# Layer 0's x and adjacency: transposed on TensorE, or loaded again as 32x32 blocks and turned on VectorE

## Chip, core and metric

The kernel runs on one core of one Trainium2 chip. The metric is the device time of an execution in microseconds (us). Engines are named as in the profile: PE (TensorE, PEld its weight loads), DVE (VectorE), ACT (ScalarE), POOL (GpSimd) and SP (SyncE, which issues the DMAs).

## What is computed

128 graphs of 128 nodes with 512 features each, float32, go through two graph attention layers with 8 heads of 64. `x` is [128, 128, 512], `adj` is [128, 128, 128].

```python
# layer 0
Q, K, V = x @ W_q + b_q, x @ W_k + b_k, x @ W_v + b_v          # split into 8 heads
scores = Q K^T / sqrt(64) + (x @ w_g[:D])[:, :, None] + (x @ w_g[D:])[:, None, :] + b_g + log(adj + 1e-9)
x = softmax(scores) V + x
# layer 1
q, k, v = x @ Wq.T + bq, x @ Wk.T + bk, x @ Wv.T + bv
logits = q k^T / sqrt(64) + log(max(adj, 1e-8))
out = (softmax(logits) v) @ Wo.T + bo
x = layer_norm(x + out) * gamma + beta
```

## The kernel before

**Groups and steps.** The work goes in groups of G = 4 graphs, 32 groups. For every group and layer `proj_units` makes the projections (features on the partitions for q and k, nodes on the partitions for v), and `attn_units` the attention of each of the four graphs: `part1` computes the scores of 8 heads, transposed (keys on the partitions), the exponential on ACT (L216) and the product with the transposed adjacency on DVE (L223), so that the log becomes a factor; `part2` does the weighted sum with a column of ones for the denominator (L233) and divides (L250 to L257); `part3`, in layer 1 only, transposes the result (L272), multiplies by Wo (L277), adds x1 (L279) and does the layer norm, with its statistics and scaling on DVE (L305, L307, L311) and the rest on POOL (L309, L310, L312, L313), and stores the graph's output.

**The order.** The loop at L290 has one step for each group `s`, in two halves. In the first half the projections of group `s` in layer 0 are merged, unit by unit, with the attention of group `s - 2` in layer 1; then group `s + 1` is loaded (`load`); in the second half the projections of group `s - 1` in layer 1 are merged with the attention of group `s` in layer 0. This is the order in which the program is written. A scheduler then orders each engine's instructions, by dependence and its own estimates, and hands out the buffers of the pools; each engine works through its own list in that order, and an instruction that waits holds up all behind it on its engine.

**Transposes of the inputs.** The projections need x with features on the partitions, and the product at L223 needs the adjacency transposed. In `transposed` PE turns four 128x128 blocks of x into a PSUM tile (`ptx`, L123), and DVE copies the tile to `xT` (L124): four such units per group and layer. `adjacency` (layer 0 only) turns the four graphs' adjacency (`padj`, L129), and DVE reads that PSUM tile twice, into the two layers' factors in `adjT` (L131, L132). In layer 1, L123 and L124 transpose x1, the result of layer 0.

**Buffers.** `xT` has two buffers, which both layers share; `x` has two, `adj` two, `adjT` three. PSUM: two buffers `tr` for transposes, two `proj` for projections, Wo and v, one for the scores, one for the weighted sums.

**DMA.** SP issues all loads and stores. Group 0 is loaded first, then the weights and biases, then the other groups as buffers come free.

After the groups a count of good denominators decides whether a general path runs again; with these inputs it doesn't.

Of the kernel before, what the change touches and what calls it, by code (L numbers as in the profile page):

```python
# [8 lines left out]
F32 = mybir.dt.float32  # L9
# [3 lines left out]
AX = mybir.AxisListType  # L13
PSUM = bass.MemoryType.PSUM

H, P, G = 8, 128, 4
EPS0, ADJ_MIN, LN_EPS = 1e-9, 1e-8, 1e-5


# [3 lines left out]
def merged(a, b):  # L23

    order = [((i + 0.5) / len(a), 0, u) for i, u in enumerate(a)]
    order += [((i + 0.5) / len(b), 1, u) for i, u in enumerate(b)]
    return [u for _, _, u in sorted(order, key=lambda x: x[:2])]


def weight(nc, pool, w, name):  # L30
    KC = w.shape[0] // P
    t = pool.tile([P, KC, w.shape[1]], F32, name=name)
    nc.sync.dma_start(t, w.rearrange("(c p) e -> p c e", p=P))
    return t
# [14 lines left out]
def fast_path(ctx, tc, args, GOOD):  # L49
# [9 lines left out]
    nc = tc.nc  # L59
    B, N, D = x.shape  # L60
    HD = D // H
    KC = D // P
    NG = B // G
# [4 lines left out]
    act = ctx.enter_context(tc.tile_pool(name="act", bufs=2))  # L68
    work = ctx.enter_context(tc.tile_pool(name="work", bufs=2))
    small = ctx.enter_context(tc.tile_pool(name="small", bufs=4))  # L70
    ps = ctx.enter_context(tc.tile_pool(name="ps", bufs=2, space=PSUM))

    X, ADJ, AT2 = {}, {}, {}

    def load(g):
        X[g] = act.tile([P, G, D], F32, tag="x", name=f"x_{g}")
        nc.sync.dma_start(X[g], x[g * G : (g + 1) * G].rearrange("b p d -> p b d"))
        ADJ[g] = act.tile([P, G, N], F32, tag="adj", name=f"adj_{g}")
        nc.sync.dma_start(ADJ[g], adj[g * G : (g + 1) * G].rearrange("b p j -> p b j"))

    ident = const.tile([P, P], F32, name="ident")
    make_identity(nc, ident)

    load(0)
    WQ, WK, BQ, BK, BV = {}, {}, {}, {}, {}
    WQ[0], WK[0] = weight(nc, const, w_q0, "wq0"), weight(nc, const, w_k0, "wk0")

# [13 lines left out]
    minus_half = const.tile([P, 1], F32, name="minus_half")  # L101
    nc.gpsimd.memset(minus_half, -0.5)

    XT, X1, QT, KT, V, AC, GATE, PT, AT, RC = {}, {}, {}, {}, {}, {}, {}, {}, {}, {}

    def proj_units(g, L):
        src = X if L == 0 else X1

        def start():
            XT[g, L] = act.tile([P, KC, G, N], F32, tag="xT", name=f"xT_{g}_{L}")  # L110
            QT[g, L] = act.tile([P, KC, G, N], F32, tag="qT", name=f"qT_{g}_{L}")
            KT[g, L] = act.tile([P, KC, G, N], F32, tag="kT", name=f"kT_{g}_{L}")
            V[g, L] = act.tile([P, G, H, HD + 1], F32, tag="v", name=f"v_{g}_{L}")
            nc.gpsimd.memset(V[g, L][:, :, :, HD : HD + 1], 1.0)
            if L == 0:
                AC[g] = small.tile([P, G, 2], F32, tag="ac", name=f"ac_{g}", bufs=2)

        def transposed(c):
            if c == 0:
                start()  # L120
            p = ps.tile([P, G, N], F32, tag="tr", name=f"ptx_{g}_{L}_{c}")
            for b in range(G):
                nc.tensor.transpose(p[:, b, :], src[g][:, b, c * P : (c + 1) * P], ident)  # L123
            nc.vector.tensor_copy(XT[g, L][:, c], p)  # L124

        def adjacency():
            p = ps.tile([P, G, N], F32, tag="tr", name=f"padj_{g}")
            for b in range(G):
                nc.tensor.transpose(p[:, b, :], ADJ[g][:, b], ident)  # L129
            AT2[g] = act.tile([P, 2, G, N], F32, tag="adjT", name=f"adjT_{g}", bufs=3)  # L130
            nc.vector.tensor_scalar_add(AT2[g][:, 0], p, EPS0)  # L131
            nc.vector.tensor_scalar_max(AT2[g][:, 1], p, ADJ_MIN)  # L132

        def qk(W, bias, dst, e):
            p = ps.tile([P, G * N], F32, tag="proj", name=f"pqk_{g}_{L}_{e}")
            for c in range(KC):
                nc.tensor.matmul(  # L137
                    p,
                    W[L][:, c, e * P : (e + 1) * P],
                    XT[g, L][:, c].rearrange("p b n -> p (b n)"),  # L140
                    start=(c == 0),
                    stop=(c == KC - 1),
                )
            nc.scalar.activation(  # L144
                dst[g, L][:, e].rearrange("p b n -> p (b n)"), p, AF.Identity, bias=bias[L][:, e : e + 1]
            )

        def v0(b, s):
            W2 = D // 2
            n = W2 + 2 * s  # L150
            p = ps.tile([P, W2 + 2], F32, tag="proj", name=f"pv_{g}_{L}_{b}_{s}")
            for c in range(KC):
                nc.tensor.matmul(  # L153
                    p[:, 0:n], XT[g, L][:, c, b], wv0[:, c, s * W2 : s * W2 + n],
                    start=(c == 0), stop=(c == KC - 1),
                )
            h2 = slice(s * H // 2, (s + 1) * H // 2)
            nc.vector.tensor_tensor(
                V[g, L][:, b, h2, 0:HD],
                p[:, 0:W2].rearrange("p (h d) -> p h d", d=HD),  # L160
                BV[L][:, s * W2 : (s + 1) * W2].rearrange("p (h d) -> p h d", d=HD),
                ALU.add,
            )
            if s == 1:
                nc.vector.tensor_copy(AC[g][:, b], p[:, W2:n])

        def v1(b):
            p = ps.tile([P, D], F32, tag="proj", name=f"pv_{g}_{L}_{b}")
            for c in range(KC):
                nc.tensor.matmul(p, XT[g, L][:, c, b], wv1[:, c], start=(c == 0), stop=(c == KC - 1))  # L170
            nc.vector.tensor_tensor(
                V[g, L][:, b, :, 0:HD],
                p.rearrange("p (h d) -> p h d", h=H),
                BV[L].rearrange("p (h d) -> p h d", h=H),
                ALU.add,
            )

        def gate():

            GATE[g] = small.tile([P, G, 1], F32, tag="gate", name=f"gate_{g}", bufs=2)  # L180
            nc.scalar.activation(GATE[g], AC[g][:, :, 0:1], AF.Exp, bias=bg)

        def add_bo():
            for b in range(G):
                nc.gpsimd.tensor_tensor(X1[g][:, b], X1[g][:, b], BO, ALU.add)

        u = [lambda c=c: transposed(c) for c in range(KC)]
        if L == 0:
            u += [adjacency]
        for e in range(KC):  # L190
            u += [lambda e=e: qk(WQ, BQ, QT, e), lambda e=e: qk(WK, BK, KT, e)]
        if L == 0:
            u += [lambda b=b, s=s: v0(b, s) for b in range(G) for s in range(2)]
            u += [gate]
        else:
            u += [add_bo]
            u += [lambda b=b: v1(b) for b in range(G)]
        return u
# [91 lines left out]
    for s in range(NG + 2):  # L290
        a = proj_units(s, 0) if s < NG else []
        b = attn_units(s - 2, 1) if s >= 2 else []
        for u in merged(a, b):
            u()
        if s + 1 < NG:
            load(s + 1)
        a = proj_units(s - 1, 1) if 1 <= s <= NG else []
        b = attn_units(s, 0) if s < NG else []
        for u in merged(a, b):
            u()  # L300


# [166 lines left out]
@with_exitstack  # L469
def kernel(ctx: ExitStack, tc: tile.TileContext, *args):  # L470

    nc = tc.nc
    B = args[0].shape[0]
    keep = ctx.enter_context(tc.tile_pool(name="keep", bufs=1))
    GOOD = keep.tile([P, 2 * B // G], F32, name="good")
    bad = keep.tile([1, 1], I32, name="bad")
    with ExitStack() as inner:
        fast_path(inner, tc, args, GOOD)
    with ExitStack() as inner:
        any_bad(inner, tc, GOOD, 2 * B * H * P, bad)  # L480
    again = nc.values_load(
        bad[0:1, 0:1], min_val=0, max_val=1, skip_runtime_bounds_check_because="a comparison's 0 or 1"
    )
    with tc.If(again > 0):
        with ExitStack() as inner:
            general_path(inner, tc, args)
# [32 lines left out]
```

## Time and profile before

| | |
|---|---|
| Time, median of 2 runs (lowest, highest) | 4115.93 us (4115.29, 4116.58) |
| The profiled execution's own time | 4108.59 us |
| Its span on the core | 4106.8 us |
| Clock granted to PE | 0.999 |
| Moved by DMA | 86.90 MB in 60141 packets |
| Length of a step in the steady state | 127.39 us |

The profile is of one execution. A row of a timeline or group gives the source line, engine and operation, what is written and read, the shape and, with x, how many; "128x512 f32" is 128 partitions of 512 elements. Matmuls are pipelined, so that a row's length overlaps with the next; the distance from start to start tells what one costs. A float32 matmul counts as two records, a transpose as one. "<-" behind a row names what ended the idle time before it. The chain of work follows the last instruction back to the first, at each step to what released it.

### The profile page before, as it was taken

To read this page: it belongs to the slowest core of one execution; us is meant where nothing else is said; L and a number is where in the kernel's file an instruction comes from. 1 tells how busy PE (TensorE), PEld (TensorE's weight loads), DVE (VectorE), ACT (ScalarE), POOL (GpSimd) and SP (SyncE) were. 2 spreads that over 40 slices of the span, in tenths; PEclk is the share of its full clock that TensorE was granted. 3 is DMA by queue.
4 is the path that set the end of the run, shared out by engine and by line. 5 is a ranking of instruction groups with operands and counts; after the bars stand their busy time and mean duration, and the time that the engine had idled before them with its cause. 6 is when DMAs were issued, how large, how long until landed. Compare 5 with 4: busy or idle time off the path is not lost.

```text
span 4106.8 us, 42009 instructions
## 1 busy us (share of the span) xinstructions
PE 4079.4 (99%) x18050; PEld 2428.7 (59%) x18050; DVE 1298.8 (32%) x2563; ACT 705.3 (17%) x929; POOL 810.2 (20%) x839
## 2 busy tenths in 40 slices
PE   9999999999999999999999999999999999999998
PEld 5565665656656566556665565655656556565564
DVE  2232322323223233233332332323323233232333
ACT  1111112111121111111111111111111111111111
POOL 0122211222112221122211222212222012221123
PEclk9999999999999999999999999999999999999999
DMA  3000000000000000000000000000000000000000
GB/s 126 13 24 11 24 19 19 23 11 24 19 19 24 11 24 21 16 24 13 21 21 18 21 21 13 24 16 21 24 11 24 16 21 24 11 24 16 6 11 21
DMA packets 60141, 86.90 MB, mean 21 GB/s; under 512 B 6576, under 2 KB 22960, under 8 KB 59952
## 3 DMA queue, kind: packets, MB, share of 16 engines
q1 hardware_dynamic: 59952, 84.17, 6.0%
q8 instruction: 144, 2.36, 0.2%
q14 instruction: 45, 0.37, 0.0%
HBM read 50.61 MB, written 33.55 MB: 20 GB/s over the span
## 4 chain that ended last, share of the span: by engine, by line
PE 99%; DVE 0%; SPq 0%; POOL 0%; DMA 0%; ACT 0%; issue 0%; ACTq 0%; POOLq 0%; DVEq 0%
PE pqk L137 43%; PE po L277 11%; PE pv L170 11%; PE pv L153 11%; PE av L233 11%; PE s L208 7%; PE ptx L123 3%; PE pta L272 1%; PE padj L129 0%; DMA bq<-in_L_gnn_b_q_dram 0%; DVE t L223 0%; SPq L91 0%; ACT aT L274 0%; DVE h L311 0%; POOL h L312 0%
## 5 line engine op out<-in xcount | busy, mean ns | idle before, releaser
L137 PE MATMUL pqk<-xT,wq 128*128 128x512 f32 x2048 | 936.0, 595 | 0.9 <-DVE xT L124 0.7
L137 PE MATMUL pqk<-xT,wk 128*128 128x512 f32 x2048 | 935.2, 599 | 0.0
L137 PEld LDWEIGHTS pqk<-xT,wq 128*128 128x128 f32 x2048 | 374.3, 190 | 418.9 <-issue 382.9
L137 PEld LDWEIGHTS pqk<-xT,wk 128*128 128x128 f32 x2048 | 374.6, 190 | 413.3 <-issue 402.3
L223 DVE TENSOR_TENSOR t<-t,adjT 128x1024 f32<-128x1024 f32 x256 | 313.4, 1224 | 797.0 <-ACT t L216 797.0
L233 PEld LDWEIGHTS av<-v,t 128*128 128x128 f32 x4096 | 494.4, 192 | 95.4 <-issue 90.4
L233 PE MATMUL av<-v,t 128*128 128x65 f32 x4096 | 485.7, 272 | 3.1 <-DVE at L257 2.0
L153 PE MATMUL pv<-wv,xT 128*128 128x256 f32 (+1 forms) x2048 | 470.2, 380 | 0.0
L277 PE MATMUL po<-wo,aT 128*128 128x512 f32 x1024 | 466.7, 599 | 1.3 <-ACT aT L274 1.3
L170 PE MATMUL pv<-wv,xT 128*128 128x512 f32 x1024 | 461.4, 599 | 0.0
L153 PEld LDWEIGHTS pv<-wv,xT 128*128 128x128 f32 x2048 | 385.2, 189 | 106.4 <-issue 58.4
L309 POOL TENSOR_SCALAR rs<-mv 128x1 f32<-128x1 f32 x128 | 28.5, 223 | 1959.5 <-DVE mv L307 1959.5
L264 POOL TENSOR_TENSOR x<-x,x 128x512 f32<-128x512 f32 x128 | 161.8, 1264 | 1001.7 <-DVE x L257 1001.7
L208 PEld LDWEIGHTS s<-qT,kT 64*128 64x128 f32 x4096 | 259.4, 187 | 164.3 <-issue 114.7
L208 PE MATMUL s<-qT,kT 64*128 64x128 f32 x4096 | 319.9, 286 | 2.4 <-ACT t L216 2.4
L144 ACT ACTIVATE kT<-pqk,bk 128x512 f32<-128x512 f32 x256 | 175.9, 687 | 848.3 <-PE pqk L137 848.3
L144 ACT ACTIVATE qT<-pqk,bq 128x512 f32<-128x512 f32 x256 | 176.0, 687 | 796.0 <-PE pqk L137 796.0
L170 PEld LDWEIGHTS pv<-wv,xT 128*128 128x128 f32 x1024 | 187.3, 190 | 204.2 <-issue 200.4
L277 PEld LDWEIGHTS po<-wo,aT 128*128 128x128 f32 x1024 | 188.8, 189 | 197.9 <-issue 184.7
L216 ACT ACTIVATE t<-s 128x1024 f32<-128x1024 f32 x128 | 131.2, 1025 | 665.4 <-PE s L208 662.9
L279 DVE TENSOR_TENSOR h<-po,x 128x512 f32<-128x512 f32 x128 | 88.5, 691 | 436.7 <-PE po L277 436.7
L312 POOL TENSOR_TENSOR h<-h,gamma 128x512 f32<-128x512 f32 x128 | 190.0, 1485 | 83.9 <-DVE h L311 64.1
(44 smaller groups left out, 2042.1 us busy)
## 6 DMA issues: line engine op xcount, KB each, us to landing
x<-in_x_dram SPq DMA_DIRECT2D x32, 1024.0 KB, 5.3
out_dram<-h SPq DMA_DIRECT2D x128, 256.0 KB, 2.0
adj<-in_adj_dram SPq DMA_DIRECT2D x32, 256.0 KB, 2.8
wq<-in_L_gnn_W_q_dram SPq DMA_DIRECT2D x1, 1024.0 KB, 8.1
wk<-in_L_gnn_W_k_dram SPq DMA_DIRECT2D x1, 1024.0 KB, 10.3
wv<-in_L_gnn_W_v_dram SPq DMA_DIRECT2D x1, 1024.0 KB, 12.5
wq<-in_L_gnn_Wq_dram SPq DMA_DIRECT2D x1, 1024.0 KB, 7.9
wk<-in_L_gnn_Wk_dram SPq DMA_DIRECT2D x1, 1024.0 KB, 10.1
```

The costliest lines, as they stand in the source:

```text
L123: nc.tensor.transpose(p[:, b, :], src[g][:, b, c * P : (c + 1) * P], ident)
L137: nc.tensor.matmul(p, W[L][:, c, e * P : (e + 1) * P], XT[g, L][:, c].rearrange("p b n -> p (b n)"), start=(c == 0), stop=(c == KC - 1),)
L144: nc.scalar.activation(dst[g, L][:, e].rearrange("p b n -> p (b n)"), p, AF.Identity, bias=bias[L][:, e : e + 1])
L153: nc.tensor.matmul(p[:, 0:n], XT[g, L][:, c, b], wv0[:, c, s * W2 : s * W2 + n], start=(c == 0), stop=(c == KC - 1),)
L170: nc.tensor.matmul(p, XT[g, L][:, c, b], wv1[:, c], start=(c == 0), stop=(c == KC - 1))
L208: nc.tensor.matmul(s[:, r, c], KT[g, L][r * HD : (r + 1) * HD, c, b], QT[g, L][r * HD : (r + 1) * HD, c, b], start=True, stop=True,)
L216: nc.scalar.activation(t, s.rearrange("p r c j -> p (r c) j"), AF.Exp, scale=SCALE, **({"bias": AC[g][:, b, 1:2]} if L == 0 else {}),)
L223: nc.vector.tensor_tensor(t, t, AT2[g][:, L, b : b + 1, :].to_broadcast([P, H, N]), ALU.mult)
L233: nc.tensor.matmul(a4[:, h // KC, h % KC], t[:, (h % 2) * KC + h // 2], V[g, L][:, b, h], start=True, stop=True,)
L264: nc.gpsimd.tensor_tensor(dst, dst, X[g][:, b], ALU.add)
L277: nc.tensor.matmul(po, aT[:, c], WO[:, c], start=(c == 0), stop=(c == KC - 1))
L312: nc.gpsimd.tensor_tensor(h, h, GA, ALU.mult)
```

## The change

x is loaded twice: once as before (for the residual), and a second time in pieces of 32 floats. Seen as 32x32 blocks, block (node block t, feature block 4c + q) is put at partition block q, column block t of chunk c of `xT`: the blocks are in transposed place, and inside a block nothing is turned yet. DVE then transposes each 32x32 block in place (`nc.vector.transpose`), 128x512 at a time. The adjacency is loaded only in this way, into the second half of `adjT`, turned in place, and scaled from there into both halves. For each group that is four DMAs for x and four for the adjacency, one of each for every 32 partitions, in place of one for the adjacency; every contiguous piece is 128 bytes. The transposes on PE of layer 0's x and of the adjacency, their PSUM tiles and the DVE copies are gone. `xT` and `adjT` of a group are now allocated at its load, a step earlier; the tile `adj` is gone. In the loop the five turning units of group `s + 1` are written into the second half, one after every second unit from unit 14 on.

```diff
     def load(g):
         X[g] = act.tile([P, G, D], F32, tag="x", name=f"x_{g}")
         nc.sync.dma_start(X[g], x[g * G : (g + 1) * G].rearrange("b p d -> p b d"))
-        ADJ[g] = act.tile([P, G, N], F32, tag="adj", name=f"adj_{g}")
-        nc.sync.dma_start(ADJ[g], adj[g * G : (g + 1) * G].rearrange("b p j -> p b j"))
+        XT[g, 0] = act.tile([P, KC, G, N], F32, tag="xT", name=f"xT_{g}_0")
+        AT2[g] = act.tile([P, 2, G, N], F32, tag="adjT", name=f"adjT_{g}", bufs=3)
+        xs = x[g * G : (g + 1) * G].rearrange("b (t i) (c q f) -> q i c (b t) f", i=S, q=P // S, f=S)
+        adjs = adj[g * G : (g + 1) * G].rearrange("b (t i) (q f) -> q i (b t) f", i=S, f=S)
+        for q in range(P // S):
+            rows = slice(q * S, (q + 1) * S)
+            nc.sync.dma_start(
+                XT[g, 0][rows].rearrange("i c b (t f) -> i c (b t) f", f=S), xs[q]
+            )
+            nc.sync.dma_start(
+                AT2[g][rows, 1].rearrange("i b (t f) -> i (b t) f", f=S), adjs[q]
+            )
+
+    def turn_units(g):
+        def features(c):
+            t = XT[g, 0][:, c].rearrange("p b n -> p (b n)")
+            nc.vector.transpose(t, t)
+
+        def adjacency():
+            a = AT2[g].rearrange("p l b n -> p l (b n)")
+            nc.vector.transpose(a[:, 1], a[:, 1])
+            nc.vector.tensor_scalar_add(a[:, 0], a[:, 1], EPS0)
+            nc.vector.tensor_scalar_max(a[:, 1], a[:, 1], ADJ_MIN)
+
+        return [lambda c=c: features(c) for c in range(KC)] + [adjacency]
...
     load(0)
+    for u in turn_units(0):
+        u()
...
         def transposed(c):
-            if c == 0:
-                start()
             p = ps.tile([P, G, N], F32, tag="tr", name=f"ptx_{g}_{L}_{c}")
             for b in range(G):
-                nc.tensor.transpose(p[:, b, :], src[g][:, b, c * P : (c + 1) * P], ident)
+                nc.tensor.transpose(p[:, b, :], X1[g][:, b, c * P : (c + 1) * P], ident)
             nc.vector.tensor_copy(XT[g, L][:, c], p)
-
-        def adjacency():
-            p = ps.tile([P, G, N], F32, tag="tr", name=f"padj_{g}")
-            for b in range(G):
-                nc.tensor.transpose(p[:, b, :], ADJ[g][:, b], ident)
-            AT2[g] = act.tile([P, 2, G, N], F32, tag="adjT", name=f"adjT_{g}", bufs=3)
-            nc.vector.tensor_scalar_add(AT2[g][:, 0], p, EPS0)
-            nc.vector.tensor_scalar_max(AT2[g][:, 1], p, ADJ_MIN)
...
-        u = [lambda c=c: transposed(c) for c in range(KC)]
-        if L == 0:
-            u += [adjacency]
+        u = [start]
+        if L == 1:
+            u += [lambda c=c: transposed(c) for c in range(KC)]
...
-        for u in merged(a, b):
+
+        turn = turn_units(s + 1) if s + 1 < NG else []
+        for i, u in enumerate(merged(a, b)):
+            u()
+            if turn and i >= 14 and i % 2 == 0:
+                turn.pop(0)()
+        for u in turn:
             u()
```

More of the change, by code (lines that the diff above doesn't have):

```diff
@@ L14 @@
 PSUM = bass.MemoryType.PSUM
-H, P, G = 8, 128, 4
+H, P, G, S = 8, 128, 4, 32
 EPS0, ADJ_MIN, LN_EPS = 1e-9, 1e-8, 1e-5
@@ L71, in fast_path @@
     ps = ctx.enter_context(tc.tile_pool(name="ps", bufs=2, space=PSUM))
-    X, ADJ, AT2 = {}, {}, {}
+    X, XT, AT2 = {}, {}, {}
     def load(g):
@@ L102, in fast_path @@
     nc.gpsimd.memset(minus_half, -0.5)
-    XT, X1, QT, KT, V, AC, GATE, PT, AT, RC = {}, {}, {}, {}, {}, {}, {}, {}, {}, {}
+    X1, QT, KT, V, AC, GATE, PT, AT, RC = {}, {}, {}, {}, {}, {}, {}, {}, {}
     def proj_units(g, L):
-        src = X if L == 0 else X1
         def start():
-            XT[g, L] = act.tile([P, KC, G, N], F32, tag="xT", name=f"xT_{g}_{L}")
+            if L == 1:
+                XT[g, 1] = act.tile([P, KC, G, N], F32, tag="xT", name=f"xT_{g}_1")
             QT[g, L] = act.tile([P, KC, G, N], F32, tag="qT", name=f"qT_{g}_{L}")
@@ L185, in add_bo @@
                 nc.gpsimd.tensor_tensor(X1[g][:, b], X1[g][:, b], BO, ALU.add)
-        u = [lambda c=c: transposed(c) for c in range(KC)]
-        if L == 0:
-            u += [adjacency]
+        u = [start]
+        if L == 1:
+            u += [lambda c=c: transposed(c) for c in range(KC)]
         for e in range(KC):
```

## The prediction

> **What bounds the kernel now.** I read the page's busy times and chain of work first, then TensorE's timeline over one group of four batches, then VectorE's at the same place, the chain of the first 75 us, and SyncE's waits.
>
> ```profile
> PE 4079.4 (99%) x18050; PEld 2428.7 (59%) x18050; DVE 1298.8 (32%) x2563; ACT 705.3 (17%) x929; POOL 810.2 (20%) x839
> PE pqk L137 43%; PE po L277 11%; PE pv L170 11%; PE pv L153 11%; PE av L233 11%; PE s L208 7%; PE ptx L123 3%; PE pta L272 1%; PE padj L129 0%; DMA bq<-in_L_gnn_b_q_dram 0%; DVE t L223 0%; SPq L91 0%; ACT aT L274 0%; DVE h L311 0%; POOL h L312 0%
> ```
>
> TensorE is the bound: 4079.4 of 4106.8 us, and the chain is nearly all TensorE. So work taken off it is worth its time if nothing new makes it wait. A group's step takes 127.39 us (the same matmuls start at 1019.52 and at 1146.91). The first half of a step, layer 0's projections among layer 1's attention, opens like this on TensorE:
>
> ```profile
> 1184.50 0.60 PE L123 MATMUL ptx<-ident,x 128*128 128x128 f32 x4
> 1185.03 1.16 PE L208 MATMUL s<-qT,kT 64*128 64x128 f32 x16
> 1186.12 1.09 PE L123 MATMUL ptx<-ident,x 128*128 128x128 f32 x8
> 1187.05 1.02 PE L137 MATMUL pqk<-xT,wq 128*128 128x512 f32 x2
> 1188.00 1.16 PE L208 MATMUL s<-qT,kT 64*128 64x128 f32 x16
> 1189.10 0.65 PE L123 MATMUL ptx<-ident,x 128*128 128x128 f32 x4
> 1189.59 0.60 PE L129 MATMUL padj<-ident,adj 128*128 128x128 f32 x4
> 1190.03 1.90 PE L233 MATMUL av<-v,t 128*128 128x65 f32 x16
> ```
>
> Matmuls overlap, so I take the distance to the next row's start and not the mean of 273 ns: 0.53 + 0.93 + 0.49 + 0.44 = 2.39 us a step for the 20 transposes that go. The page's 3% cannot be used whole: L123 is layer 1's transposes too, and those stay.
>
> The second half, layer 1's projections among layer 0's attention, opens like this on TensorE, and then on VectorE:
>
> ```profile
> 1129.55 0.60 PE L123 MATMUL ptx<-ident,x 128*128 128x128 f32 x4
> 1130.08 0.94 PE L208 MATMUL s<-qT,kT 64*128 64x128 f32 x12
> 1130.95 1.09 PE L123 MATMUL ptx<-ident,x 128*128 128x128 f32 x8
> 1131.87 1.02 PE L137 MATMUL pqk<-xT,wq 128*128 128x512 f32 x2
> 1132.83 1.16 PE L208 MATMUL s<-qT,kT 64*128 64x128 f32 x16
> 1133.92 0.66 PE L123 MATMUL ptx<-ident,x 128*128 128x128 f32 x4
> ```
>
> ```profile
> 1129.75 0.69 DVE L279 TENSOR_TENSOR h<-po,x 128x512 f32<-128x512 f32 x1 [2.94 <-PE po L277]
> 1130.36 0.68 DVE L124 COPY xT<-ptx 128x512 f32<-128x512 f32 x1
> 1130.95 0.68 DVE L305 BATCH_NORM_STATS2 st<-h 128x6 f32<-128x512 f32 x1
> 1131.67 0.18 DVE L307 BATCH_NORM_AGGREGATE mv<-st 128x2 f32<-128x6 f32 x1
> 1131.77 0.66 DVE L124 COPY xT<-ptx 128x512 f32<-128x512 f32 x1
> 1132.85 0.55 DVE L311 TENSOR_SCALAR h<-h,mv,rs 128x512 f32<-128x512 f32 x1 [0.42 <-POOL rs L310]
> 1133.31 1.22 DVE L223 TENSOR_TENSOR t<-t,adjT 128x1024 f32<-128x1024 f32 x1
> ```
>
> TensorE has no gap here, because the first two copies of xT slip in ahead of the last layer norm's scaling (L311), which has to wait for POOL. The change touches exactly this order.
>
> ```profile
> 8.91 7.45 DMA bq<-in_L_gnn_b_q_dram
> SPq L77 <- POOL x L264: 1375.6, 30, 89.2
> ```
>
> The chain's start hangs on the bias bq, last in a queue of loads; it lands at 16.36 and projections run from 18.47. In the steady state SyncE issues the next x when POOL's last add into x1 frees its buffer (at 1056.65, just before a first half).
>
> [...] adjacency's 512-byte packets take 27 ns each (0.21 of 16 engines over 4.17 us, by 512 packets), 2048-byte ones about 89 ns (1.06 of 16 engines at 389 GB/s). [...] The trace has none to compare; its nearest row, the 128x512 copy from PSUM, takes 681 ns.
>
> **The change, part by part.** Times are counted from t0, the first score matmul of a first half.
>
> TensorE loses 2.39 us a step. Group 0's transposes lay in the wait for bq and group 1's mostly in gaps of group 0's lone attention, so I count 30 groups: 30 x 2.39 = -71.7 us.
>
> VectorE loses per step four copies (4 x 0.68) and two scalings from PSUM (2 x 0.68), 4.1 us, and gains five turns and two scalings from SBUF. [...] I take 0.70. A scaling is at most L311's 0.55. Sum 4.6 us, +0.5 on an engine 32% busy. The place counts more. The built order puts the four x turns of group s+1 after group s-2's second weighted sum (at), far earlier than the loop's unit 14 suggests. TensorE gets there at t0+27.7 (three scores of 1.1, six projections of 3.5, two weighted sums of 1.73, as these rows are spaced), VectorE at 28.8, and the turns end at 31.6. Behind them stands the product for batch 3, whose exponential is not ready before 33.5 (a projection and a score to 32.3, then 0.1 and 1.02): cover 1.9 us. The adjacency turn and scalings run from 42.4 to 44.1, ahead of h (L279), which po releases at 46.1: cover 2 us. At 1.4 us a turn both covers about hold. Cost: 0.
>
> Loads: per group 8192 + 2048 packets of 128 bytes, 640 an engine, eight more issues on SyncE. [...] I take 15[...]. The built buffers give x-transposed of group s+1 the slot of layer 1's group s-2, free at t0, not the slot still in use. Landing: issue of x at t0-0.5, 1.6 to first data, 2.7 for x, 512 x 0.015 = 7.7, 1 for completion: t0+12.5, against 28.8 needed. The adjacency's issue waits for batch 3's product (34.7), and four issues at 0.45 and 2.4 to land make 39, against 42.4. Queued behind these on SyncE are only this step's four output stores, ready from 52 on. Cost 0 in the steady state. VectorE may run about 7 us late before po's buffer or h starves TensorE; so the cover is gone at a landing of t0+36, which is 4.8 + 0.512p = 36, p = 61 ns a packet.
>
> Start: these 640 packets, less adjacency's 0.9 us, go ahead of the weights and bq: 9.6 - 0.9 = +8.7 us.
>
> The moved order at the second half: the built program has the scores' last six matmuls first, then ptx 0 and 1, second score, ptx 2, one pqk, ptx 3; and on VectorE h, statistics, aggregate, scaling (waits for POOL), only then copy 0, product, copy 1, copy 2, product, copy 3. From P, po's end: h at P+0.20, statistics 0.92, aggregate 1.65, scaling 2.83 (the same 1.18 behind the aggregate as above), copy 0 from 3.29 to 3.97. TensorE: scores to 0.87, ptx 0 and 1 to 1.80, second score waits for the exponential until 2.16 (+0.36) and ends at 3.25; ptx 2 waits for copy 0's PSUM buffer until 4.04 (+0.79); pqk to 5.41; ptx 3 waits for copy 1, behind a 1.14 product, until 5.78 (+0.37); the last pqk waits until 8.12 for copy 3 and ends at 9.0. Before, the same work took 1129.55 to 1137.01 = 7.46. So +1.54 us a step, 30 x 1.54 = +46.2 us.
>
> Sum on the profiled execution: 4106.8 - 71.7 + 46.2 + 8.7 = 4090.0. The median of the runs, 4115.93, stands 9.1 above that span: 4099 us.
>
> **Rivals.** (a) No new wait: if the copies keep up with TensorE, 4106.8 - 71.7 + 8.7 + 9.1 = 4053 us, 1.5% faster. For it: the wait is built from sub-microsecond gaps. Against: the built order. (b) Slower, by late loads: VectorE stands at the turns with the product, v and h behind it. At p = 40 the start alone (+16 more) cancels the gain; from 61 every step stalls 0.512 us per further ns; at p = 65 it is 2% slower; at 80, 30 x 9.7 + 50 - 9 makes about 4430 us. For it: [...] no 128-byte packet in this trace. Against: 512 bytes take 27 ns. (c) Between: p of 27 to 60, or turns above 1.4 us, 4110 to 4190 us. (d) The transposes weren't what TensorE waited on, so nothing is gained: excluded by its 99%.
>
> **How the numbers follow.** New wait and loads in time: 0.50, own range 4078 to 4118. No new wait: 0.18, 4045 to 4062. Between: 0.17. Late: 0.12. A gain over 2% (under 4033.6) would need more than the whole 71.7 us and a free start: 0.03. The range 4045 to 4145 holds the first two and over half of the third, and cuts the late loads off. Two per cent is about what a measurement of this kernel can tell from no change: faster 0.03, same 0.82, slower 0.15.
>
> **What would show it.** Right: no x transposes of layer 0 on TensorE, a step of about 126.5 us, gaps before ptx 2, ptx 3 and the last pqk with releaser xT's copy, turns with no DMA before them, first projections some 9 us later. Wrong: turns waiting on DMA, turns far above 0.7 us, steps of 125.0 us, or scores waiting elsewhere.

## The result, and the profile after

| | before | after |
|---|---|---|
| Time, median of 2 runs (lowest, highest) | 4115.93 us (4115.29, 4116.58) | 4167.11 us (4167.01, 4167.21) |
| The profiled execution's own time, and its span | 4108.59, 4106.8 us | 4167.21, 4165.4 us |
| Length of a steady step | 127.39 us | 128.69 us |
| Start of group 1's value projections in layer 0 | 96.36 us | 113.79 us |

The kernel became slower: the ratio of the times is 1.0133, with a 95% interval of 1.0109 to 1.0158. The forecast was 4099 us, a little faster than before. First the busy times and the start of the chain of work on the page of the changed kernel:

```profile
PE 4039.2 (97%) x17410; PEld 2364.4 (57%) x17410; DVE 1341.5 (32%) x2595; ACT 705.0 (17%) x929; POOL 809.8 (19%) x839
...
PE 92%; DVE 7%; POOL 1%; issue 0%; SPq 0%; ACT 0%; DMA 0%; POOLq 0%; ACTq 0%; DVEq 0%
```

TensorE lost 4079.4 - 4039.2 = 40.2 us of busy time and 640 transposes (18050 to 17410), yet the span grew by 58.6 us. The chain that was all TensorE now runs 7% of the span through VectorE. The waits of TensorE say where. The columns are the total, the number of times and the longest:

```profile
PE ptx L146 <- DVE xT L147: 47.2, 62, 0.9
PE pqk L152 <- DVE xT L147: 32.5, 31, 1.1
```

Two times in every step a transpose of layer 1, and once a projection, waits for VectorE's copy of xT. The place is the opening of the second half, which the prediction shows for the kernel before. After the change TensorE's timeline reads so:

```profile
1154.43 0.94 PE L223 MATMUL s<-qT,kT 64*128 64x128 f32 x12
1155.30 1.09 PE L146 MATMUL ptx<-ident,x 128*128 128x128 f32 x8
1156.59 1.16 PE L223 MATMUL s<-qT,kT 64*128 64x128 f32 x16 [0.19 <-ACT t L231]
1158.37 0.66 PE L146 MATMUL ptx<-ident,x 128*128 128x128 f32 x4 [0.63 <-DVE xT L147]
1158.87 1.02 PE L152 MATMUL pqk<-xT,wq 128*128 128x512 f32 x2
1160.80 0.66 PE L146 MATMUL ptx<-ident,x 128*128 128x128 f32 x4 [0.91 <-DVE xT L147]
1161.29 1.88 PE L152 MATMUL pqk<-xT,wq 128*128 128x512 f32 x4
1164.24 1.12 PE L152 MATMUL pqk<-xT,wq 128*128 128x512 f32 x2 [1.06 <-DVE xT L147]
1165.20 1.90 PE L248 MATMUL av<-v,t 128*128 128x65 f32 x16
```

The order is the forecast one (scores first, then two units of ptx), and so are the four waits. But the piece takes 1165.20 - 1154.43 = 10.77 us where it took 7.46: +3.31 us a step, not +1.54. VectorE and POOL in the same microseconds, from the timeline of all engines:

```profile
1157.80 1.27 POOL L333 TENSOR_TENSOR h<-h,gamma 128x512 f32<-128x512 f32 x1 [0.66 <-DVE h L332]
1158.24 1.91 DVE L238 TENSOR_TENSOR t<-t,adjT 128x1024 f32<-128x1024 f32 x1
...
1161.24 4.69 POOL L200 TENSOR_TENSOR x<-x,bo 128x512 f32<-128x512 f32 x3
1161.27 2.31 DVE L238 TENSOR_TENSOR t<-t,adjT 128x1024 f32<-128x1024 f32 x1
```

Look at the two products (L238): 1.91 and 2.31 us instead of 1.22, together 1.78 us more, which is the 1.77 us that the forecast is short of. Neither has a bracket with a wait: the time hides inside the instruction. Each time a POOL product or addition in SBUF began shortly before (1157.80 and 1161.24). In the kernel before the same pair met the other way round. Its product at 1133.31 (shown in the prediction) came first and took 1.22 us, and POOL paid:

```profile
1133.47 2.19 POOL L312 TENSOR_TENSOR h<-h,gamma 128x512 f32<-128x512 f32 x1 [0.66 <-DVE h L311]
```

So the theory was: the moved order costs 3.31 us a step, of which some 1.5 are waits that the order makes by itself, and some 1.8 come from products that now start after POOL's work and stand still until it ends. Rivals: the block loads or the turns slow the step; the products are slow for another reason.

The account of the whole: 30 x (-2.10 in the first half, +3.31 at the opening, +0.09 in the rest of the second half) = +39 us, the start +17.4 us (96.36 to 113.79), some 2 us left over: 58.6 us. Most of these 2 us can be a short stretch near the end, in which TensorE's granted clock is lower: 0.92 on average from 4050 to 4055 us and 0.74 to 4060. That is worth up to 1.7 us (an estimate: 0.08 x 5 + 0.26 x 5). In the kernel before the clock is 1.00 until the last 10 us.

### The profile page after: what moved, and what is told of

Its sections match the earlier page's. It is cut to its first block, busy times and chain, and to the rows that moved or that the text cites. A ratio compares the mean times of both kernels' runs of the same rounds, so it can differ in the third digit from the quotient of the medians.

```text
span 4165.4 us, 41178 instructions
## 1 busy us (share of the span) xinstructions
PE 4039.2 (97%) x17410; PEld 2364.4 (57%) x17410; DVE 1341.5 (32%) x2595; ACT 705.0 (17%) x929; POOL 809.8 (19%) x839
## 4 chain that ended last, share of the span: by engine, by line
PE 92%; DVE 7%; POOL 1%; issue 0%; SPq 0%; ACT 0%; DMA 0%; POOLq 0%; ACTq 0%; DVEq 0%
PE pqk L152 42%; PE av L248 11%; PE po L292 11%; PE pv L168 11%; PE pv L185 11%; PE s L223 6%; DVE t L238 3%; DVE xT L147 2%; PE pta L287 1%; DVE st L326 1%; DVE h L294 1%; POOL rs L331 0%; DVE h L332 0%; SPq L88 0%; POOL rs L330 0%
## 5 line engine op out<-in xcount | busy, mean ns | idle before, releaser
L152 PE MATMUL pqk<-xT,wq 128*128 128x512 f32 x2048 | 946.2, 600 | 50.6 <-DVE xT L147 32.5
L238 DVE TENSOR_TENSOR t<-t,adjT 128x1024 f32<-128x1024 f32 x256 | 366.9, 1433 | 850.3 <-ACT t L231 850.3
L186 DVE TENSOR_TENSOR v<-pv,bv 128x512 f32<-128x512 f32 x128 | 88.4, 691 | 389.8 <-PE pv L185 389.8
```

Of the source, the lines that this page charges most:

```text
L152: nc.tensor.matmul(p, W[L][:, c, e * P : (e + 1) * P], XT[g, L][:, c].rearrange("p b n -> p (b n)"), start=(c == 0), stop=(c == KC - 1),)
L186: nc.vector.tensor_tensor(V[g, L][:, b, :, 0:HD], p.rearrange("p (h d) -> p h d", h=H), BV[L].rearrange("p (h d) -> p h d", h=H), ALU.add,)
L238: nc.vector.tensor_tensor(t, t, AT2[g][:, L, b : b + 1, :].to_broadcast([P, H, N]), ALU.mult)
```

## Experiments

The kernel before measured 4110.03, 4109.99 and 4109.71 us in the three sets below, against 4115.93 us in the runs above. So times are compared by their ratio to the kernel before of the same set, and traces by the length of a step. The changed kernel's own values are 1.0133 and 128.69 us.

**The order put back, the change kept.**

```diff
+            if c == 0:
+                start()
             p = ps.tile([P, G, N], F32, tag="tr", name=f"ptx_{g}_{L}_{c}")
...
         if L == 1:
-            u += [lambda c=c: transposed(c) for c in range(KC)]
+            u = [lambda c=c: transposed(c) for c in range(KC)]
```

The change made `start` a unit of its own, so that layer 1's list has 18 units and not 17. `merged` sorts units by (i + 0.5) / length: the first transposing unit moves from 0.029 to 0.083, and the first scores, at 0.0625, overtake it.

> The change is kept whole (block loads, turns, no transposes of layer 0 on TensorE); only the opening of layer 1's projections is put back inside its first transposed unit, as before, so that this list has 17 units and not 18. The built order at the opening of the second half is then the one of the kernel before. Theory (the changed order, with the contention it brings, cost 3.31 us a step): step 128.69 - 3.3 = about 125.4 us, opening back at 7.5 us, time about 4167 - 30 x 3.3 = 4068 us. Rival (the loads, or the turns on VectorE, slow the step, whatever the order): step stays at about 128.7, time about 4167 us.

Measured: 4062.63 us, ratio 0.9883 (0.9866 to 0.9899), step 125.30 us. The same place again:

```profile
1132.21 1.22 DVE L240 TENSOR_TENSOR t<-t,adjT 128x1024 f32<-128x1024 f32 x1
1132.37 2.18 POOL L335 TENSOR_TENSOR h<-h,gamma 128x512 f32<-128x512 f32 x1 [0.66 <-DVE h L334]
```

The transposes come first again, at 1128.44, the weighted sum at 1135.90: the opening is back at 7.46 us, the products at 1.22, and POOL is again the one that waits. With all loads and turns in place the step is 2.09 us shorter than before: they do not slow it.

**The order alone, without the change.**

```diff
             u += [lambda b=b, s=s: v0(b, s) for b in range(G) for s in range(2)]
             u += [gate]
         else:
+            u = [lambda: None] + u
             u += [add_bo]
```

> The kernel before with nothing but one empty unit in front of layer 1's list of projections: no block loads, no turns, all 20 transposes on TensorE. The order at the opening of the second half becomes that of the changed kernel. Theory (the order alone, with its contention, costs 3.3 us a step): step 127.39 + 3.3 = 130.7 us, time about 4116 + 30 x 3.3 = 4215 us. Rival 1 (the order costs the forecast 1.54 us and the rest comes from loads and turns): about 4162 us. Rival 2 (the order is harmless): 4116 us.

Measured: 4218.04 us, ratio 1.0260 (1.0243 to 1.0277), step 130.78 us, which is 3.39 more than before. An empty unit that issues no instruction costs what the theory says. The opening's first and last row, and the group of the products, whose mean was 1224 ns in the kernel before:

```profile
1154.52 0.94 PE L210 MATMUL s<-qT,kT 64*128 64x128 f32 x12
1165.28 1.90 PE L235 MATMUL av<-v,t 128*128 128x65 f32 x16
...
L225 DVE TENSOR_TENSOR t<-t,adjT 128x1024 f32<-128x1024 f32 x256 | 368.0, 1438 | 821.4 <-ACT t L218 821.4
```

The opening takes 10.76 us, as in the changed kernel. The rival with the forecast 1.54 us falls.

**POOL's part of it.** From here on the edits are to the changed kernel, except in the probes.

```diff
             for b in range(G):
-                nc.gpsimd.tensor_tensor(X1[g][:, b], X1[g][:, b], BO, ALU.add)
+                pass
...
-    nc.gpsimd.tensor_tensor(h, h, GA, ALU.mult)
-    nc.gpsimd.tensor_tensor(h, h, BE, ALU.add)
```

> The changed kernel with three additions and products of GpSimd left out: the bias of the output projection is not added to x1, and layer norm ends without gamma and beta. The order and the waits of the opening stay those of the changed kernel. Theory (the products of VectorE are stretched from 1.22 to 1.91 and 2.31 us by GpSimd's work on SBUF beside them): the two products at the opening fall back to about 1.2 us, the opening from 10.77 to about 9.0 us, step about 126.9 us, time about 4167 - 30 x 1.77 = 4114 us. Rival (they are slow for another reason, the loads' writes to SBUF or the turns): products stay near 1.9 and 2.3 us, time about 4167 us.

Measured: 4108.89 us, ratio 0.9995 (0.9986 to 1.0004), step 126.88 us. On VectorE's timeline both products stand at their old length, in the changed order:

```profile
1146.26 1.21 DVE L238 TENSOR_TENSOR t<-t,adjT 128x1024 f32<-128x1024 f32 x1
1147.39 1.28 DVE L147 COPY xT<-ptx 128x512 f32<-128x512 f32 x2
1148.59 1.22 DVE L238 TENSOR_TENSOR t<-t,adjT 128x1024 f32<-128x1024 f32 x1
```

The opening takes 1151.42 - 1142.47 = 8.95 us. So of the 3.31 us, 8.95 - 7.46 = 1.49 belong to the order as such, and 10.77 - 8.95 = 1.82 to POOL.

**Which POOL instruction holds which product.** A first try moved the unit that adds the bias behind the value projections.

```diff
-            u += [add_bo]
             u += [lambda b=b: v1(b) for b in range(G)]
+            u += [add_bo]
```

> The changed kernel with one unit moved: the four additions of the output bias on GpSimd come after the four value projections of layer 1, not before them. Theory (each stretched product is slowed by the very GpSimd instruction that started just before it): the second product at the opening starts 0.03 us after the first addition of the bias, so without this addition it falls from 2.31 to about 1.22 us, while the first product, beside the multiplication by gamma, stays at 1.91 us; step 128.69 - 1.1 = 127.6 us, time about 4134 us. Rival (the second product is slowed by the tail of what started earlier, or by GpSimd's presence in general): it stays near 2.3 us, time about 4167 us.

Measured: 4167.12 us, ratio 1.0135 (1.0119 to 1.0152), step 128.64 us. This tells nothing on the theory: POOL still does the addition right behind beta (at 1158.55, the product at 1158.59 takes 2.31), because the scheduler put it there all the same. In the next run these additions alone were left out.

> The changed kernel with the four additions of the output bias to x1 on GpSimd left out (gamma and beta stay; the bias is not added). In the run that moved this unit, the order on GpSimd came out as it was, so it told nothing on the second product. Theory (the second product waits for the first of these additions, which starts 0.03 us before it): the second product falls from 2.31 to about 1.22 us, the first stays at 1.91 us, the wait of the last projection for the fourth copy goes (1.06 us), step 128.69 - 1.1 = 127.6 us, span about 4134 us. Rival (it waits for what started earlier, the addition of beta): it stays near 2.3 us, span about 4167 us.

Measured: 4133.17 us, ratio 1.0054 (1.0037 to 1.0070), span 4132.0 us, step 127.59 us. Both engines:

```profile
1150.82 1.27 POOL L333 TENSOR_TENSOR h<-h,gamma 128x512 f32<-128x512 f32 x1 [0.66 <-DVE h L332]
1151.25 1.91 DVE L238 TENSOR_TENSOR t<-t,adjT 128x1024 f32<-128x1024 f32 x1
...
1154.29 1.21 DVE L238 TENSOR_TENSOR t<-t,adjT 128x1024 f32<-128x1024 f32 x1
```

The first product still waits for gamma; the second, with no POOL product or addition running beside it (beta ends as it starts), takes 1.21 us. Each stretch belongs to one neighbour, and 128.69 - 127.59 = 1.10 us is the second one's share.

**The meeting by itself.** Probes ahead of the kernel before: four VectorE instructions, each alone, then with a small POOL instruction and a long one (128x512, in SBUF) after its start, then with the long one started 0.15 us before it.

```python
product: nc.vector.tensor_tensor(d, d, m, ALU.mult)                       # 128x1024, all in SBUF
turn:    nc.vector.transpose(d[:, 0:512], d[:, 0:512])
scaling: nc.vector.tensor_scalar_add(d[:, 0:512], d[:, 0:512], EPS0)
bank:    nc.vector.tensor_tensor(d[:, 0:512], q, m[:, 0:512], ALU.mult)   # q in PSUM
```

> The kernel before with a row of probes ahead of it: four VectorE instructions (a product 128x1024 with both inputs in SBUF, a turn 128x512, a scaling 128x512, a product 128x512 with one input in PSUM) are run four times each alone, four times started shortly before a GpSimd product 128x512 in SBUF, and four times shortly after it. Theory (the one that starts first keeps its speed, the other waits): the product takes 1.22 us alone and first, about 1.9 to 2.4 us second; GpSimd takes 1.27 us alone and first, about 2.2 us second. Rival 1 (both are slowed alike whichever starts first): about 1.9 us in both orders. Rival 2 (VectorE always wins): 1.22 us in all three. For the turn, the scaling and the product from PSUM no number is known: alone 0.68, 0.43 and 0.69 us.

The time of this single run (4241.08 us) says nothing; its trace does. The groups, with the number of instructions, busy time and mean ns. L321 and L324 are the product first and second (alone, L318, its mean is 1220); L339 and L342 the scaling first and second; L333 the turn second, L351 the product from PSUM second:

```profile
L324 DVE TENSOR_TENSOR pd<-pd,pm 128x1024 f32<-128x1024 f32 x4 | 8.8, 2192 | 0.1
L342 DVE TENSOR_SCALAR pd<-pd 128x512 f32<-128x512 f32 x4 | 5.6, 1395 | 0.1
...
L321 DVE TENSOR_TENSOR pd<-pd,pm 128x1024 f32<-128x1024 f32 x4 | 4.9, 1225 | 0.1
...
L333 DVE STREAM_TRANSPOSE pd<-pd 128x512 f32<-128x512 f32 x4 | 2.8, 711 | 0.1
...
L351 DVE TENSOR_TENSOR pd<-pq,pm 128x512 f32<-128x512 f32 x4 | 2.8, 692 | 0.1
...
L339 DVE TENSOR_SCALAR pd<-pd 128x512 f32<-128x512 f32 x4 | 1.7, 426 | 0.1
```

The product takes 1.22 us alone and first, 2.19 second; the scaling 0.43 first and 1.40 second. The turn and the product from PSUM don't change (711 and 692 ns in all three cases). One product that started second:

```profile
32.99 1.26 POOL L357 TENSOR_TENSOR pg<-pg,pn 128x512 f32<-128x512 f32 x1
33.14 2.19 DVE L324 TENSOR_TENSOR pd<-pd,pm 128x1024 f32<-128x1024 f32 x1
```

The lengths fit a second one that stops altogether. When the product starts, POOL's instruction has 1.11 us to go here, 0.83 us at gamma in the changed kernel and 1.23 us at the bias (its median of 1.26 us taken). The product becomes longer by 0.97, 0.69 and 1.09 us, each time 0.14 us less than that.

POOL pays in the same way, and here it is the small instruction at the head that does, not the long one behind it for which about 2.2 us had been expected. One such pair:

```profile
19.09 1.22 DVE L321 TENSOR_TENSOR pd<-pd,pm 128x1024 f32<-128x1024 f32 x1
19.20 1.17 POOL L363 TENSOR_TENSOR pg<-pfp 128x1 f32<-128x1 f32 x1 [0.53 <-DVE pfp L363]
```

One element per partition takes POOL 0.19 us elsewhere and 1.17 here, until the product is done. Who starts first keeps its speed (1.22 us for the product, 1.26 for POOL's long instruction) and the other stands still (2.19 us for the product, 1.17 for POOL's small one): both rivals fall.

**The loads and the turns.** The second copies loaded as rows of 512 bytes in their own places:

```diff
-                XT[g, 0][rows].rearrange("i c b (t f) -> i c (b t) f", f=S), xs[q]
+                XT[g, 0][rows], x[g * G : (g + 1) * G, rows].rearrange("b i (c f) -> i c b f", f=P)
...
-                AT2[g][rows, 1].rearrange("i b (t f) -> i (b t) f", f=S), adjs[q]
+                AT2[g][rows, 1], adj[g * G : (g + 1) * G, rows].rearrange("b i f -> i b f")
```

> The changed kernel, but the second copies of x and adjacency are loaded in their own places, in rows of 512 bytes, and not in 32x32 blocks of 128-byte rows; the same number of transfers and bytes, a quarter of the packets, the turns kept. (What is computed is another function of x: layer 0 works on features and tokens left unexchanged between blocks.) Theory (in the steady steps the small packets are hidden; they cost only at the start): step stays at 128.7 us, the first projection starts some 6 to 9 us earlier, time about 4159 us. Rival (three times as many packets slow the step itself, by late loads or by traffic into SBUF beside VectorE): step falls by 1 us or more, time under 4135 us.

Measured: 4155.06 us, ratio 1.0110 (1.0093 to 1.0127), step 128.70 us. A quarter of the packets, with the same bytes, leaves the step and the products (mean 1437 ns) alone, so the number of packets is not what slows them. The start gains 11.9 us of span, but not as expected. The first projection comes at 15.24 us in place of 18.08, only 2.8 us earlier (and at 20.56 in the run without turns below, whose loads are the changed kernel's, so single traces differ by nearly as much). The rest is at group 1, whose first projection starts at 60.66 us and not at 84.64.

The turns left out:

```diff
-            nc.vector.transpose(t, t)
+            pass
...
-            nc.vector.transpose(a[:, 1], a[:, 1])
```

> The changed kernel with the five turns of each group left out on VectorE (block loads and the two scalings of adjacency stay; layer 0 works on blocks that are in transposed place but not turned). Theory (turns are hidden in the steady steps; at the start group 1's turns stand behind group 0's attention on VectorE and hold up group 1's projections): step stays at 128.7 us, group 1's first v comes up to 8.5 us earlier, time about 4157 us. Rival (the turns' 3.4 us a step on VectorE lengthen the step): step about 126 us or less, time under 4100 us.

Measured: 4166.66 us, ratio 1.0132 (1.0116 to 1.0149), step 128.70 us. The turns are hidden in the steady step, as forecast; the rival falls. But the theory on the start falls too: group 1's first projection starts at 82.81 us even with no turn ahead of it. The projections' first rows of group 1, one from each trace (rows of 512 bytes, no turns):

```profile
60.66 1.98 PE L150 MATMUL pqk<-xT,wq 128*128 128x512 f32 x4
```

```profile
82.81 1.91 PE L151 MATMUL pqk<-xT,wq 128*128 128x512 f32 x2
```

What differs is the built order on TensorE. With block loads it puts group 1's projections behind all of group 0's scores and behind three or all four of its weighted sums; with rows of 512 bytes it spreads them among these. That the scheduler reckons small packets as late, and orders by that, is a guess of mine that no run tried by itself.

The order is not the whole of it: in the changed kernel TensorE's granted clock is 0.50 from 71 to 87 us. In the kernel before it is 1.00 all through the start. The same weighted sum, in the kernel before and in the changed one:

```profile
70.53 1.90 PE L233 MATMUL av<-v,t 128*128 128x65 f32 x16
```

```profile
76.05 3.52 PE L248 MATMUL av<-v,t 128*128 128x65 f32 x16
```

From the start of group 0's value projections to that of group 1's it takes 65.70 us instead of 57.19. An estimate of the 8.5 us: some 17 us at half the clock, with 1.2 us of them idle, cost about 8; gaps of TensorE in group 0's attention cost 4.2 us in place of 1.0; the transposes that are gone give 2.4 back. The runs with the order put back, without POOL's work, without turns and with the bias moved have such a stretch too: in it weighted sums take up to 3.62, 3.65, 3.65 and 3.65 us. With rows of 512 bytes they take 1.90 to 1.97 us. The gaps come first: from 60 to 71 us TensorE is busy for 8.0 us in the changed kernel, for 10.3 us in the kernel before and with rows of 512 bytes. Whether the gaps bring the clock down was not shown: no run tries the clock and the order apart.

**The best version: the order kept, groups 0 and 1 brought in as before.**

```diff
+        if g < 2:
+            nc.sync.dma_start(AT2[g][:, 0], adj[g * G : (g + 1) * G].rearrange("b p j -> p b j"))
+            return
...
-        if L == 1:
+        if L == 1 or g < 2:
             u = [lambda c=c: transposed(c) for c in range(KC)]
+            if L == 0:
+                u += [adjacency]
```

(`transposed` takes x for layer 0, `adjacency` is that of before, the turns begin with group 2, and the order of the first experiment is in it.)

> The order kept as in the first experiment, and groups 0 and 1 brought in as before (plain loads, transposes on TensorE), block loads and turns for groups 2 to 31 only. Theory: the start of before (group 1's first v at 96.5 us, not 114), 28 steps shorter by the 2.1 us that the first half gained: 4116 - 28 x 2.1 = about 4057 us, some 10 to 17 us below the first experiment. Rival (the late start was given back later anyway, or came from somewhere else): equal to the first experiment, about 4068 us.

Measured: 4045.81 us, ratio 0.9842 (0.9825 to 0.9858), step 125.29 us, span 4044.1 us. It is 15.4 us of span below the first experiment: group 1's value projections start at 96.46 us, not at 112.47, and group 0's weighted sums take 1.90 to 2.00 us, as in the kernel before. On its page TensorE is the bound again, busy for 4016.3 us, 99% of the span.

It beats both kernels, 1.6% below the one before.

## Why the prediction was wrong

- **The transposes on TensorE.** Forecast -2.39 us a step, measured 70.34 against 72.44 us in the first half: -2.10, or -63 us in 30 steps and not -71.7. Reading distances from start to start was the right price; the page's 3% would have been far off. The missing 0.29 us is spread over rows that stand a little further apart beside new neighbours: in sum 0.15 us at the projections of q and k, 0.10 at Wo's product and 0.06 at the values.
- **The moved order: the step that failed.** The prediction had "ptx 3 waits for copy 1, behind a 1.14 product" and summed the moved order to "+1.54 us a step". Order, place and releasers came out as said, but the two products take 1.91 and 2.31 us. The term was worth +3.31 us a step, so +99 us and not +46.2. With POOL's products and additions out of the way it is +1.49, so the waits themselves had been sized well. I had placed VectorE's instructions on a line of their own and looked at POOL only as the one to be waited for, never as a neighbour. The trace of before held the warning: POOL's multiplication by gamma at 1133.47 took 2.19 us under a VectorE product, and its mean was 1485 ns where the bias's addition had 1272. I didn't ask which of the two would pay once the order turned round. The probes answer it: the product takes 1.22 us when it starts first and 2.19 when it starts second. The added loads don't stretch it: with all of them in place the first experiment's products have the mean of the kernel before, 1224 ns.
- **The start.** Forecast +8.7 us for the packets ahead of the weights; group 0's value projections start at 48.09 and not at 39.17: +8.9. The size was right by luck, since it was reckoned from the packets alone: with a quarter of the packets they still start at 45.60, 6.4 us later than before. There wq's issue, at 1.78 us before, stands at 7.64 us, behind the eight issues on SyncE that took the place of one (12.03 in the changed kernel). And 8.5 us more come from group 1, which the prediction let lie "mostly in gaps". It asked neither where group 1's projections would stand once its transposes were gone, nor what would fill the gaps of group 0's lone attention then. These projections no longer do, the gaps grow, and the granted clock is 0.50 behind them. By the estimate above the clock is the greater part.
- **Loads.** Hidden, as forecast. With a quarter of the packets the step stays at 128.70 us. A 128-byte packet costs 14.4 ns, by the changed kernel's trace, against the assumed 15, an estimate that the trace of before could not show (over 1083.54 to 1096.00 the engines are busy 0.82 of the time: 163.5 engine-us, less 512 x 89 ns for x's long packets, by 8192). Turns wait for a DMA only at the start (13.8 us, once).
- **Turns.** 677 ns for x, 698 for the adjacency, against 0.70 assumed, an estimate near the 681 ns of the copy from PSUM, since the trace of before has no turn; hidden, as the run without them shows (128.70 us a step).
- **The rivals.** "No new wait" at 4053 us is what the change does when the order is kept: 4062.63. Late loads did not come. No rival had the meeting of VectorE and POOL; the measured time lies in the range of "between", for a reason that wasn't named there.

With the measured sizes, 4106.8 - 63 + 99 + 17.4 is 4160 us, against a span of 4165.4; the rest of the second half adds 2.7 us (30 x 0.09). In the span the forecast was 75.4 us short (4090.0), and 53 of them are the opening's (30 x 1.77). The medians lie only 68 us apart, which is luck: the forecast added 9.1 us from span to median, and for the changed kernel that distance is 1.7 us (4167.11 - 4165.4).

## What to carry to other kernels

Where a change moves instructions, lay VectorE's and POOL's timelines side by side and ask for each pair that meets in SBUF who starts first: the second one can stand still inside its own duration (2.19 us in place of 1.22), with no wait in the profile. It mattered here only where others waited for that engine: POOL's gamma at 2.19 us left the opening at 7.46 us. Look at means that differ for one shape on one engine; here they were meetings that already happened. And a unit that issues nothing can still reorder the program when the order is a sort by position: compare the built orders and give the change the old one before judging it.

## What was not expected of the hardware

- The stretch depends on the operands: beside a POOL product in SBUF, a VectorE product from SBUF goes from 1.22 to 2.19 us and a scaling from SBUF from 0.43 to 1.40, while the 32x32 turn (0.71) and a product with one input in PSUM (0.69) stay.
- It hits the smallest POOL instruction as well: 128x1 takes 1.17 us in place of 0.19.
